# Two row combinations of a Winograd convolution move from GpSimd to VectorE

## The chip, the cores and the metric

The kernel runs on one core of a Trainium2 chip. A core has five engines with instruction queues of their own: TensorE (PE in the profile; PEld is its weight loading), VectorE (DVE), ScalarE (ACT), GpSimd (POOL) and SyncE (SP), which here only issues transfers. All tensors are float32. The metric is the time on the device in microseconds, as the median of several runs.

## The reference, cut to what matters

Four layers run one after the other on `x` of shape 2 x 128 x 128 x 128 (image, channel, row, column). Layers 0 and 2 are a 3x3 convolution followed by a small state-space recurrence and a group normalisation, layer 1 is a gating by local density. The change lies in layer 3, a basic block:

```
w1b = w1 + lax.stop_gradient(jnp.sign(w1) - w1)
w2b = w2 + lax.stop_gradient(jnp.sign(w2) - w2)
out = jax.nn.relu(_batchnorm(_conv3x3(x, w1b), gamma1, beta1))
out = _batchnorm(_conv3x3(out, w2b), gamma2, beta2)
out = out + x
return jax.nn.relu(out)
```

`_batchnorm` needs mean and variance over both images, so the first convolution has to be complete before the second begins. The input of layer 3 is the output of layer 2, `x + silu(groupnorm(...))`, and the kernel makes this sum band by band inside the first convolution.

## The kernel before, in words

Layer 3 is `_basic_block`. Channels lie on the 128 partitions. The 2 x 128 rows are cut into 32 bands of 8 rows (`BAND`), each two groups of four rows (`fours`). A band tile `xb` has 10 rows of 130 columns; three of them (`room`) are used in turn.

The 3x3 convolution is done by a Winograd scheme along the rows. For four output rows, six input rows are turned into six combinations (`comb`, the tile `v` of 6 x 2 x 130 elements a partition), each is multiplied by three weight matrices (one for each column tap) on TensorE, and the six products are put together into four output rows.

The combinations are made in three functions:

- `edges` (L889): VectorE makes four of them as `high - 4 * low` from rows of the band, one instruction of 260 elements each, and puts them at positions 0, 3, 2 and 5 of `v`.
- `differences`: GpSimd makes the two outer combinations in one instruction of 520 elements (L895: position 2 minus 0 and position 5 minus 3, written to 0 and 5), then a sum in place at position 3 (L896), then the differences at positions 1 and 4 straight from the band (L897).
- `rest_of` (L901 to L903): VectorE finishes positions 4, 1 and 2 from these.

`products` (L910) is the 18 matrix products of a band into `m` in PSUM (36 records in the profile). `conv` puts them together: ScalarE copies one third to `c` (L921), VectorE does four sums and differences (L925, L926), five steps into the result `Y` (L930 to L934) and two statistics (L936). `m` has two buffers in PSUM and `v` three in SBUF.

In the first convolution each band also has: `load` on SyncE's queue (L980 for the band, L982 for the residual's operand), and `residual`: ScalarE's Silu on the band (L988), GpSimd's addition of the residual (L989, 1280 elements), and SyncE's store of the sum (L990). In the second convolution there is `normalised` instead: GpSimd copies two rows (L1001) and ScalarE does the rest (L1003).

`convolve` writes the order out by hand for all five engines (`manual_schedule`): each engine gets its instructions in the order of the text. Step `k` finishes the combinations of band `k+1`, begins those of `k+2`, multiplies band `k`, puts band `k-1` together, and on GpSimd does the operations of `differences` for band `k+2` and then the residual of band `k+3`.

Of the kernel before, what the change touches and what calls it, by code (L numbers as in the profile page):

```python
# [27 lines left out]
ALU = mybir.AluOpType  # L28
# [791 lines left out]
def _basic_block(tc, src, y, norm, x3, scratch, w1, w2, bn, out, B, H):  # L820
# [7 lines left out]
    nc = tc.nc  # L828
    fours = BAND // 4
    with tc.tile_pool(name="bb", bufs=1) as cp, tc.tile_pool(name="bband", bufs=2) as bp, tc.tile_pool(  # L830
# [3 lines left out]
        def combined():  # L834
            return bp.tile([P, 6, fours, P + 2], F32, tag="comb", name="comb", bufs=3)
# [35 lines left out]
        def span(k):  # L871

            r0 = bands[k][1]
            return room[k % 3], 1 if r0 == 0 else 0, BAND + 1 if r0 + BAND == H else BAND + 2

        def border(k):
# [3 lines left out]
            if hi == BAND + 1:  # L880
                nc.gpsimd.memset(xb[:, BAND + 1, :], 0.0)

        def edges(k):

            xb = span(k)[0]
            v = combined()
            low, high = [xb[:, n : n + BAND, :].rearrange("p (i n) w -> p n i w", n=4) for n in (0, 2)]
            for n, at in enumerate((0, 3, 2, 5)):
                nc.vector.scalar_tensor_tensor(v[:, at], low[:, n], -4.0, high[:, n], ALU.mult, ALU.add)  # L889
            return v  # L890

        def differences(k, v):
            xb = span(k)[0]
            low, high = [xb[:, n : n + BAND, :].rearrange("p (i n) w -> p n i w", n=4) for n in (0, 2)]
            nc.gpsimd.tensor_tensor(v[:, 0:6:5], v[:, 2:6:3], v[:, 0:4:3], ALU.subtract)  # L895
            nc.gpsimd.tensor_tensor(v[:, 3], v[:, 2], v[:, 3], ALU.add)  # L896
            nc.gpsimd.tensor_tensor(v[:, 1:5:3], high[:, 1:3], low[:, 1:3], ALU.subtract)  # L897

        def rest_of(v):
            x = [v[:, n].rearrange("p i w -> p (i w)") for n in range(6)]  # L900
            nc.vector.scalar_tensor_tensor(x[4], x[1], -2.0, x[4], ALU.mult, ALU.add)  # L901
            nc.vector.scalar_tensor_tensor(x[1], x[1], 4.0, x[4], ALU.mult, ALU.add)
            nc.vector.scalar_tensor_tensor(x[2], x[2], 2.0, x[3], ALU.mult, ALU.subtract)  # L903

        def products(v):

            m = pp.tile([P, 3, 2, fours, P], F32, tag="m", name="m")
            for n, i in enumerate((2, 4, 3, 1, 0, 5)):
                for kw in range(3):
                    nc.tensor.matmul(  # L910
                        m[:, n // 2, n % 2],
                        lhsT=u[:, i, kw, :],
                        rhs=v[:, i, :, kw : kw + P],
                        start=(kw == 0),
                        stop=(kw == 2),
                    )
            return m

        def conv(m, b, r0, stats):
            c = bp.tile([P, 2, fours, P], F32, tag="c", name="c")  # L920
            nc.scalar.copy(c, m[:, 0])  # L921
            sd1 = bp.tile([P, 2, fours, P], F32, tag="sd", name="sd", bufs=1)
            sd2 = pp.tile([P, 2, fours, P], F32, tag="sd", name="sd")
            for n, sd in enumerate((sd1, sd2)):
                nc.vector.tensor_tensor(sd[:, 0], m[:, 1, n], c[:, n], ALU.add)  # L925
                nc.vector.tensor_tensor(sd[:, 1], m[:, 1, n], c[:, n], ALU.subtract)  # L926
            rows = Y[:, b, r0 : r0 + BAND, :]
            y = rows.rearrange("p (i n) w -> p n i w", n=4)
            (s1, d1), (s2, d2) = [(sd[:, 0], sd[:, 1]) for sd in (sd1, sd2)]
            nc.vector.tensor_tensor(y[:, 0:4:3], m[:, 2], sd1, ALU.add)  # L930
            nc.vector.scalar_tensor_tensor(y[:, 1], d2, 2.0, d1, ALU.mult, ALU.add)
            nc.vector.scalar_tensor_tensor(y[:, 2], s2, 4.0, s1, ALU.mult, ALU.add)
            nc.vector.tensor_tensor(y[:, 0], s2, y[:, 0], ALU.add)
            nc.vector.scalar_tensor_tensor(y[:, 3], d2, 8.0, y[:, 3], ALU.mult, ALU.add)  # L934
            for n in range(BAND // ROWS):
                nc.vector.bn_stats(  # L936
                    stats[:, (b * H + r0) // ROWS + n, :],
                    rows[:, n * ROWS : (n + 1) * ROWS, :].rearrange("p r w -> p (r w)"),
                )

        def affine(stats, n):
            mv = cp.tile([P, 2], F32, tag=f"mv{n}", name="mv")
            nc.vector.bn_aggr(mv, stats.rearrange("p a b -> p (a b)"))
            rstd = _rstd(nc, cp, mv[:, 1:2], BN_EPS, f"bn{n}")
            return _affine(nc, cp, mv[:, 0:1], rstd, bnc[:, 2 * n : 2 * n + 1], bnc[:, 2 * n + 1 : 2 * n + 2], f"bn{n}")
# [4 lines left out]
        def convolve(load, make, n):  # L950

            stats = cp.tile([P, B * H // ROWS, 6], F32, tag="st", name="st")
            v = {}
            E = mybir.EngineType
            with tc.manual_schedule(engines={E.PE, E.Activation, E.DVE, E.Pool, E.SP}):
                m = {}
                for k in range(-4, len(bands) + 1):
                    if 0 <= k + 1 < len(bands):
                        rest_of(v[k + 1])
                    if 0 <= k + 2 < len(bands):  # L960
                        v[k + 2] = edges(k + 2)
                    if 0 <= k < len(bands):
                        m[k] = products(v.pop(k))
                    if k >= 1:
                        conv(m.pop(k - 1), *bands[k - 1], stats)
                    if 0 <= k + 2 < len(bands):
                        differences(k + 2, v[k + 2])
                    for ahead, f in ((4, load), (3, make)):
                        if 0 <= k + ahead < len(bands):
                            f(k + ahead)  # L970
            return affine(stats, n)
# [12 lines left out]
        def residual(k):  # L984
# [5 lines left out]
            nc.sync.dma_start(out=x3[b][:, r0 : r0 + BAND, :], in_=xb[:, 1 : BAND + 1, 1 : P + 1])  # L990

        s1, t1 = convolve(load, residual, 0)


# [11 lines left out]

        nc.sync.dma_start(out=u.rearrange("p a t c -> p (a t c)"), in_=later)
        s2, t2 = convolve(lambda k: None, normalised, 1)

        for k, (b, r0) in enumerate(bands):  # L1010
# [11 lines left out]
def _program(ctx, tc, d, cols, out):  # L1022
# [7 lines left out]
    with tc.tile_pool(name="const", bufs=1) as cp, tc.tile_pool(name="wts", bufs=1) as wp:  # L1030
# [24 lines left out]
        with tc.tile_pool(name="ps_n", bufs=1, space=PSUM) as pp:  # L1055
            norm = [_norm(nc, npool, pp, w, con, stats, b) for b in range(B)]
    _basic_block(tc, x2, y, norm, x3, scratch, d["L3_w1"], d["L3_w2"], d["L3_bn"], out, B, H)


# [41 lines left out]
```

## Time and profile before

| | |
|---|---|
| runs shown | 7577.68 us median of 3 (7575.1 to 7587.97) |
| the profiled execution | 7595.04 us, span 7593.2 us |
| mean granted TensorE clock | 0.929 |
| the first convolution's combinations | 6928.9 us to 7205 us of the span |
| the second convolution | 7228 us to 7490 us |

Times inside the profile are microseconds from the start of the span. A row of instructions gives busy time, mean duration in ns, and the idle time of the engine before them with what ended it. In a timeline, "x36" means 36 instructions run together into one piece, and the bracket says how long the engine sat idle before and what released it. L12 is line 12 of the kernel.

### The profile page before, as it was taken

The numbers are of one execution on the slowest core, as the hardware profiler recorded it, in microseconds if no ns is written. First come the engines' busy times: TensorE is split into PE (matmuls) and PEld (weight loads), VectorE is DVE, ScalarE is ACT, GpSimd is POOL, SyncE is SP. The second block draws the span as 40 slices with busy tenths as digits, with TensorE's granted clock in tenths as the row PEclk, the third lists the DMA queues.
The fourth block names the chain that finished last, engine by engine and source line by source line (L and its number), as shares of the span: only waits on it lengthen the run. The fifth ranks groups of instructions, "written<-read, shape, count | busy, mean of one in ns | idle before, by whom it ended". The sixth has DMA issues, their size and how long they took to land.

```text
span 7593.2 us, 89536 instructions
## 1 busy us (share of the span) xinstructions
PE 6291.6 (83%) x30416; PEld 2339.8 (31%) x30416; DVE 7026.3 (93%) x7082; ACT 4279.0 (56%) x4877; POOL 5538.6 (73%) x1815
## 2 busy tenths in 40 slices
PE   7888888888888888867888888888888888887994
PEld 2222222222222222234222222222222222224773
DVE  6999999999999999968699999999999999998986
ACT  5566656666656666545566656665666566562222
POOL 5778777877787788743687787878777877785641
PEclk8999999999999999977899999999999999997997
DMA  7999999999999999954899999999999999996604
GB/s 207 247 248 250 252 245 251 252 253 249 247 252 255 248 250 253 251 183 173 211 256 245 248 244 248 251 253 246 248 252 248 251 248 246 247 256 184 194 7 172
DMA packets 573737, 1769.79 MB, mean 233 GB/s; under 512 B 85568, under 2 KB 239712, under 8 KB 458208
## 3 DMA queue, kind: packets, MB, share of 16 engines
q1 hardware_dynamic: 568672, 1747.28, 88.1%
q10 hardware_dynamic: 4608, 16.78, 0.6%
q8 instruction: 242, 3.96, 0.2%
q14 instruction: 215, 1.76, 0.1%
HBM read 1552.83 MB, written 210.89 MB: 232 GB/s over the span
## 4 chain that ended last, share of the span: by engine, by line
DVE 39%; DMA 30%; PE 14%; issue 6%; POOL 5%; ACT 4%; SPq 2%; POOLq 0%; DVEq 0%; ACTq 0%
DMA bcr<-sb 23%; DVE set L472 12%; DVE h L477 10%; DVE r L473 10%; DMA ur<-su 4%; PE m L910 4%; POOL h L445 3%; PE set L454 2%; PE one L350 2%; ACT set L463 2%; PE ys L492 1%; PE ys L483 1%; DVE v L505 1%; PE one L400 1%; DVE comb L901 1%
## 5 line engine op out<-in xcount | busy, mean ns | idle before, releaser
L445 POOL TENSOR_TENSOR h<-ur,bcr 128x2048 f32<-128x2048 f32 x896 | 4059.2, 4537 | 1331.9 <-DMA bcr<-sb 1098.7
L472 DVE TENSOR_TENSOR set<-set,h 128x1024 f32<-128x1024 f32 x1792 | 2192.5, 1223 | 257.4 <-ACT set L463 153.8
L473 DVE TENSOR_TENSOR r<-set,bcr 128x1024 f32<-128x1024 f32 x1792 | 2194.4, 1225 | 61.4
L463 ACT ACTIVATE set<-set 128x1024 f32<-128x1024 f32 x1792 | 1743.7, 1007 | 790.0 <-PE set L454 776.4
L477 DVE TENSOR_TENSOR h<-set,h 128x1024 f32<-128x1024 f32 x1536 | 1865.4, 1214 | 43.7 <-POOL h L445 43.1
L454 PE MATMUL set<-dt,rep 32*128 32x512 f32 x7168 | 1385.9, 676 | 97.8 <-DVE h L477 93.5
L492 PE MATMUL ys<-r,ct 128*32 128x512 f32 x7168 | 1160.1, 634 | 33.0 <-DVE r L473 32.6
L323 PE MATMUL one<-band,conv 128*128 128x512 f32 x2304 | 1083.5, 606 | 22.6 <-DMA band<-in_x_dram 12.3
L400 PE MATMUL one<-xc,keep 128*64 128x512 f32 x1008 | 314.8, 707 | 470.3 <-ACT xc L357 355.8
L454 PEld LDWEIGHTS set<-dt,rep 32*128 32x128 f32 x7168 | 403.1, 193 | 977.0 <-issue 478.0
L323 PEld LDWEIGHTS one<-band,conv 128*128 128x128 f32 x2304 | 407.7, 190 | 669.1 <-issue 597.1
L910 PE MATMUL m<-comb,u 128*128 128x256 f32 x2304 | 510.2, 382 | 63.0 <-DVE comb L903 45.3
L483 PE MATMUL ys<-t,ct 128*128 128x512 f32 x512 | 324.5, 720 | 252.1 <-DVE v L505 250.5
L910 PEld LDWEIGHTS m<-comb,u 128*128 128x128 f32 x2304 | 437.5, 191 | 135.4 <-issue 72.0
L492 PEld LDWEIGHTS ys<-r,ct 128*32 128x32 f32 x7168 | 181.2, 111 | 911.3 <-issue 756.9
L352 ACT ACTIVATE xc<-one,keep 128x512 f32<-128x512 f32 x252 | 173.3, 688 | 509.7 <-PE one L350 504.8
L420 PE MATMUL one<-prod,ct 128*128 128x512 f32 x504 | 284.7, 648 | 148.4 <-POOL prod L412 126.7
L374 POOL TENSOR_TENSOR u<-dt,xc 128x1024 f32<-128x1024 f32 x128 | 302.6, 2364 | 78.1 <-ACT dt L368 77.8
L350 PE MATMUL one<-y,w_in 128*128 128x512 f32 x504 | 340.7, 765 | 1.7 <-ACT xc L352 1.7
L421 ACT COPY t<-one 128x512 f32<-128x512 f32 x252 | 147.7, 586 | 326.9 <-PE one L420 326.9
L463 ACT ACT_TABLE_LOAD x254 | 325.9, 1283 | 4.5
L427 POOL TENSOR_TENSOR t<-t,xc 128x1024 f32<-128x1024 f32 x128 | 302.1, 2360 | 10.0
(166 smaller groups left out, 6116.2 us busy)
## 6 DMA issues: line engine op xcount, KB each, us to landing
ur<-su SPq DMA_DIRECT2D x896, 896.0 KB, 11.6
bcr<-sb SPq DMA_DIRECT2D x896, 448.0 KB, 11.8
ur<-su SPq DMA_DIRECT2D x896, 128.0 KB, 11.2
su<-u SPq DMA_DIRECT2D x1024, 64.0 KB, 3.2
sb<-bc SPq DMA_DIRECT2D x256, 224.0 KB, 2.7
bcr<-sb SPq DMA_DIRECT2D x896, 64.0 KB, 11.1
y<-o SPq DMA_DIRECT2D x128, 256.0 KB, 9.2
band<-in_x_dram SPq DMA_DIRECT2D x28, 640.0 KB, 11.0
```

What stands on the lines that cost most here:

```text
L323: nc.tensor.matmul(py.rearrange("p (r w) -> p r w", r=ROWS), lhsT=w["conv"][:, tap, :], rhs=xb[:, r + kh : r + kh + ROWS, kw : kw + P], st ...
L350: nc.tensor.matmul(p, lhsT=w[("in", "z")[i]][:, g, :], rhs=s["y"], start=True, stop=True)
L400: nc.tensor.matmul(p[g * NQ * DS : (g + 1) * NQ * DS, :], lhsT=w[("xb", "xcm")[i]], rhs=s["xc"][:, g, :], start=True, stop=True,)
L445: nc.gpsimd.tensor_tensor(b, s["ur", t], s["bc", t][:, 0].unsqueeze(1).to_broadcast([P, NJ, NS]), ALU.mult)
L454: nc.tensor.matmul(a[j // 2][:, j % 2, :], lhsT=w["rep"][r, q, :], rhs=s["dt"][r, g, :], start=True, stop=True, tile_position=(r.start, 0),)
L463: nc.scalar.activation(x, x, AF.Exp)
L472: nc.vector.tensor_tensor(pt, pt, s["h", t - 1][:, js, :], ALU.mult)
L473: nc.vector.tensor_tensor(s["r", t][:, js, :], pt, s["bc", t - 1][:, 1].unsqueeze(1).to_broadcast([P, 2, NS]), ALU.mult)
L477: nc.vector.tensor_tensor(s["h", t][:, js, :], pt, s["h", t][:, js, :], ALU.add)
L483: nc.tensor.matmul(s["ys", g], lhsT=con["ident"], rhs=s["t1"][:, g, :], start=True, stop=False)
L492: nc.tensor.matmul(s["ys", g][a : a + NQ * DJ, :], lhsT=red[:, q, :], rhs=r[:, j, :], start=False, stop=(q == NQ - 1), tile_position=(0, a),)
L910: nc.tensor.matmul(m[:, n // 2, n % 2], lhsT=u[:, i, kw, :], rhs=v[:, i, :, kw : kw + P], start=(kw == 0), stop=(kw == 2),)
```

## The change

GpSimd's instruction for the two outer combinations becomes a function of its own, `outer`, which takes the engine as an argument. In the first convolution (`n == 0`) it is issued on VectorE, directly behind the four instructions of `edges`. In the second (`n > 0`) it stays on GpSimd, and GpSimd's order there is what it was: outer combinations, sum, differences. The sum at position 3 moves from `differences` to the text of the loop.

```
+        def outer(engine, v):
+            engine.tensor_tensor(v[:, 0:6:5], v[:, 2:6:3], v[:, 0:4:3], ALU.subtract)
+
...
         def differences(k, v):
             xb = span(k)[0]
             low, high = [xb[:, n : n + BAND, :].rearrange("p (i n) w -> p n i w", n=4) for n in (0, 2)]
-            nc.gpsimd.tensor_tensor(v[:, 0:6:5], v[:, 2:6:3], v[:, 0:4:3], ALU.subtract)
-            nc.gpsimd.tensor_tensor(v[:, 3], v[:, 2], v[:, 3], ALU.add)
             nc.gpsimd.tensor_tensor(v[:, 1:5:3], high[:, 1:3], low[:, 1:3], ALU.subtract)
...
                     if 0 <= k + 2 < len(bands):
                         v[k + 2] = edges(k + 2)
+                        if n == 0:
+                            outer(nc.vector, v[k + 2])
                     if 0 <= k < len(bands):
                         m[k] = products(v.pop(k))
                     if k >= 1:
                         conv(m.pop(k - 1), *bands[k - 1], stats)
                     if 0 <= k + 2 < len(bands):
+                        if n > 0:
+                            outer(nc.gpsimd, v[k + 2])
+                        nc.gpsimd.tensor_tensor(v[k + 2][:, 3], v[k + 2][:, 2], v[k + 2][:, 3], ALU.add)
                         differences(k + 2, v[k + 2])
```

More of the change, by code (lines that the diff above doesn't have):

```diff
@@ L881, in border, with outer @@
                 nc.gpsimd.memset(xb[:, BAND + 1, :], 0.0)
+        def outer(engine, v):
+            engine.tensor_tensor(v[:, 0:6:5], v[:, 2:6:3], v[:, 0:4:3], ALU.subtract)
         def edges(k):
@@ L894, in differences @@
             low, high = [xb[:, n : n + BAND, :].rearrange("p (i n) w -> p n i w", n=4) for n in (0, 2)]
-            nc.gpsimd.tensor_tensor(v[:, 0:6:5], v[:, 2:6:3], v[:, 0:4:3], ALU.subtract)
-            nc.gpsimd.tensor_tensor(v[:, 3], v[:, 2], v[:, 3], ALU.add)
             nc.gpsimd.tensor_tensor(v[:, 1:5:3], high[:, 1:3], low[:, 1:3], ALU.subtract)
@@ L961, in convolve @@
                         v[k + 2] = edges(k + 2)
+                        if n == 0:
+                            outer(nc.vector, v[k + 2])
                     if 0 <= k < len(bands):
@@ L966, in convolve @@
                     if 0 <= k + 2 < len(bands):
+                        if n > 0:
+                            outer(nc.gpsimd, v[k + 2])
+                        nc.gpsimd.tensor_tensor(v[k + 2][:, 3], v[k + 2][:, 2], v[k + 2][:, 3], ALU.add)
                         differences(k + 2, v[k + 2])
```

## The prediction

> **What bounds the kernel now.** I read four views in this order: the page's engine line, then the table of windows over the last 700 us, then the timeline of one band in each of the two convolutions, then the rows of single instructions that have the shape of the moved one.
>
> The page's engine line says that VectorE (DVE) is the busiest engine of the whole program. It does not say where; over 90% of the span belongs to other stages, which the change doesn't touch.
>
> ```profile
> PE 6291.6 (83%) x30416; PEld 2339.8 (31%) x30416; DVE 7026.3 (93%) x7082; ACT 4279.0 (56%) x4877; POOL 5538.6 (73%) x1815
> ```
>
> The windows show the stage itself. Columns: the window, its length, then busy us and count of PE, PEld, DVE, ACT and POOL, the granted PE clock, the DMA share, GB/s. The first row lies in the first convolution, the second in the second one.
>
> ```profile
> 7080.00:7100.00 20.00, 18.24 (x83) 15.13 (x82) 19.76 (x43) 4.85 (x6) 14.58 (x12) 1.00 0.76 234
> 7340.00:7360.00 20.00, 20.00 (x95) 17.53 (x94) 18.76 (x47) 3.73 (x5) 10.64 (x12) 1.00 0.00 0
> ```
>
> First convolution: DVE is full (19.76 of 20) and TensorE (PE) has gaps. Second: PE is full and DVE has gaps. Both have the same matmuls, 36 records a band, so 95 records in 20 us against 83 to 87 is the price of being bound by DVE. DVE's fullness is partly false, though, as the timeline of one band of the first convolution shows (start, duration, engine, line; DVE, POOL and PE pieces, some left out):
>
> ```profile
> 7086.01 1.44 DVE L889 SCALAR_TENSOR_TENSOR comb<-band 128x260 f32<-128x260 f32 x4
> ...
> 7087.37 0.42 DVE L925 TENSOR_TENSOR sd<-m,c 128x256 f32<-128x256 f32 x1
> 7087.60 1.29 POOL L895 TENSOR_TENSOR comb<-comb 128x520 f32<-128x520 f32 x1 [2.59 <-DVE comb L889]
> ...
> 7088.84 0.68 DVE L930 TENSOR_TENSOR Y<-m,sd 128x512 f32<-128x512 f32 x1
> 7088.97 0.73 POOL L896 TENSOR_TENSOR comb<-comb 128x260 f32<-128x260 f32 x1
> ...
> 7089.66 1.30 POOL L897 TENSOR_TENSOR comb<-band 128x520 f32<-128x520 f32 x1
> 7089.66 8.01 PE L910 MATMUL m<-comb,u 128*128 128x256 f32 x36 [0.59 <-DVE Y L930]
> ...
> 7090.91 2.69 POOL L989 TENSOR_TENSOR band<-band,xs 128x1280 f32<-128x1280 f32 x1
> ...
> 7092.08 1.81 DVE L901 SCALAR_TENSOR_TENSOR comb<-comb 128x260 f32<-128x260 f32 x1
> ...
> 7093.92 0.43 DVE L902 SCALAR_TENSOR_TENSOR comb<-comb 128x260 f32<-128x260 f32 x1
> ...
> 7094.61 1.44 DVE L889 SCALAR_TENSOR_TENSOR comb<-band 128x260 f32<-128x260 f32 x4
> ```
>
> And the same two DVE instructions in the second convolution, where GpSimd (POOL) has no residual to add:
>
> ```profile
> 7344.57 0.41 DVE L901 SCALAR_TENSOR_TENSOR comb<-comb 128x260 f32<-128x260 f32 x1
> 7345.01 0.43 DVE L902 SCALAR_TENSOR_TENSOR comb<-comb 128x260 f32<-128x260 f32 x1
> ```
>
> A band takes 8.60 us, from L889 to L889. L901 takes 0.41 us when POOL is quiet and 1.81 us here: it begins while POOL's residual L989 runs (7090.91 to 7093.60) and L902 begins 0.32 us after that ends. So of the 8.60 us, L901 to L902 is 1.84 instead of 0.44: 1.40 us a band in which DVE stands, booked as busy. PE waits for DVE (0.59 us before L910, for L930). Through this stage the chain is DVE's, and one of its links is POOL's residual, whose end is set by the three POOL operations in front of it.
>
> **The change part by part.** I count time in a band from the first L889 (7086.01 is 0). Before: L925 at 1.36, L895 at 1.59, L896 at 2.96, L897 at 3.65, L989 from 4.90 to 7.59, L901 at 6.07, L902 at 7.91, next L889 at 8.60.
>
> *Added to DVE: 32 instructions of 128x520 from two SBUF tiles.* No DVE row has just this shape; two bracket it:
>
> ```profile
> L853 DVE TENSOR_TENSOR comb<-comb 128x384 f32<-128x384 f32 x2 | 1.1, 551 | 0.0
> L847 DVE TENSOR_TENSOR comb<-comb 128x1152 f32<-128x1152 f32 x2 | 2.7, 1358 | 0.7 <-ACT comb L846 0.6
> ```
>
> (mean ns is the number behind the comma). Between them 768 elements cost 0.807 us, 1.05 ns each, so 520 elements last 0.551 + 136 x 1.05 = 0.69 us. The next instruction starts before the end of one: L930, 0.68 long, is followed after 0.60, so the queue pays 0.61. It reads what the fourth L889 wrote just before: where L902 reads what L901 wrote the step is 0.44 instead of the 0.34 between independent ones, so 0.10 more. Cost on DVE: 0.71 us a band, all of it on the chain. Nothing hides it.
>
> Here a rule of the Trainium skill speaks against the change. The page "Vector Engine (DVE) Microarchitecture Reference", section "Points that are easy to get wrong", says that the scalar_tensor_tensor with two SBUF sources that are not bf16 runs at half throughput. Taken over to this operation, that is about 0.07 + 2 x 0.54 + 0.10 = 1.25 us instead of 0.71 (an estimate from that page). The rows say otherwise: L889 is such an instruction and takes 0.42 us for 260 elements, against 0.41 for 256 in L931, which has one source in PSUM; and L847 above has two f32 SBUF sources at 1.05 ns an element. I take 0.71 and keep 1.25 as the upper end. I see no reason for less than 0.61.
>
> *Removed from POOL: L895, 1.29 us, in the first convolution only.* The sum (L896) now waits for DVE's new instruction, because it overwrites what that reads. Behind it in POOL's queue stand the difference (L897), which needs only the band, and the residual; behind the residual, SyncE's queue has the store L990 and the next band's loads L980 and L982. The new instruction runs from 1.46 to 2.15. POOL began 0.15 after the last L889's end before; the same hand-over gives 2.30 for the sum. With the old steps (0.69 from L896 to L897, 1.25 from L897 to L989) the difference starts at 2.99, the residual at 4.24, and it ends at 6.93 instead of 7.59: 0.66 us earlier.
>
> *What becomes of the stall.* L901 starts 0.71 later, at 6.78. If free, L902 follows at 7.22; behind the residual it follows at 6.93 + 0.32 = 7.25. So 1.40 us of stall shrink to 0.03, and the two conditions are nearly level. Next L889 at 7.25 + 0.69 = 7.94. The band goes from 8.60 to 7.94: **0.66 us less.** Two things moved by the same edit: 0.71 of work added, 1.37 of stall gone.
>
> A second rule bears on it: "SBUF — State Buffer", section "SBUF: two separate sides", says that a DVE instruction with two SBUF inputs and a GpSimd instruction exclude each other for the whole of whichever starts first. The L901 row above agrees. By the rule the new instruction is one more that must find POOL idle, or loses up to the residual's 2.68 us. By the timeline POOL is idle from the residual's end to the sum, 6.93 to 10.24 in the new count (the band is 7.94), and L902, L903, the four L889 and the new one all lie in it. So the rule adds nothing here, but it names the condition.
>
> *What is late next.* PE needs 7.77 us a band: in the second convolution, with PE full, L895 comes at 7347.86 and 7355.63. So 7.94 leaves PE 0.17 us of gap, and 0.66 is nearly all that can be had (0.83 at most). DMA: after L990 (7085.03) the next load goes out at 7085.49, the activation on it ends at 7092.59, and the residual that uses it comes at 7099.50: 6.9 us in hand. With the shorter band it is 2 x 0.66 less, 5.6 us. The copy L921 runs a band ahead of L925. DVE's L889 needs the comb tile of three bands back, freed by PE long before.
>
> *Ends of the stage.* The first three L901 (2.9 us each) wait for L897 and then through the residual; their bands are 8.48 and 8.51 long and become 7.94 by the same steps: 1.1 us for two, and some 0.4 for the very first, whose L901 waits for the same POOL chain. From 6957.39 to 7197.58 there are 28 whole bands: 28 x 0.66 = 18.5. In the last one that makes combinations (L889 at 7197.58) no residual remains and the 0.71 is a pure cost in front of L930, which releases PE's last 15.78 us. The second convolution keeps POOL's three operations in their order: nothing. Sum: 18.5 + 1.1 + 0.4 - 0.7 = **19.3 us.**
>
> The sum is made against the profiled execution, 7595.04 us with a span of 7593.2, which is 0.23% above the median of the runs shown. The loop that it cuts is paced by engines and not by that excess, so I take it from the median: 7577.7 - 19.3 = 7558.4, rounded to 7558.
>
> **The rivals.**
>
> *A, TensorE becomes the bound (6%).* If the new instruction pays no 0.10 for its operand and L901 comes free, DVE needs 8.60 - 1.40 + 0.61 = 7.81, and with hand-overs either engine gives about 7.8: 0.8 x 28 + 1.5 - 0.6 = 23 us, 7554. For it: the two engines are level within 0.2 us. Against: the 0.10 is in every dependent pair of the timeline.
>
> *B, part of the stall stays (8%).* The sum now waits for a different engine's last word each band. If it starts 0.35 us later than worked out, L902 is 0.35 later, the band gains 0.31: 28 x 0.31 + 1.5 - 0.7 = 9.5 us, 7568. Each 0.1 us of delay at the sum costs 2.8 us. Against: L895 has waited for DVE in the same way, always with 0.14 to 0.15.
>
> *C, the half rate of the skill's rule (5%).* 1.25 us on DVE, residual ends at 7.47, L902 at 7.79, band 8.48: 28 x 0.12 + 0.5 - 1.25 = 3 us less, 7575. Against: the rows above.
>
> *D, slower (5%): the residual is not ready when POOL comes to it.* Place: L989 waiting for the activation L988, which waits for its load. Then the residual slides onto L901 to L889 and the new instruction and holds all of them back. It decides when the residual ends later than before, so 0.66 us after the place worked out; at 1.5 us late the band is 9.44, 0.84 x 28 = 23 us more, 7601. For it: L988 waits for DMA in nearly every band already. Against: the 5.6 us in hand.
>
> That the change doesn't do what it says is little to be feared: the order on the five engines in this loop is the order of the text.
>
> **How the numbers follow.** The forecast has 76%. Its own spread is some 4 us (0.05 us a band is 1.4 us; runs shown differ by 12.9 us, a median by less). The 0.2% bound, about what a measurement of this kernel can tell from no change, is 15 us, one such spread short of 19.3, so 86% of the forecast counts as faster: 0.76 x 0.86 + 0.06 = 0.71. Within: 0.76 x 0.14 + 0.08 + 0.05 = 0.24. Slower: 0.05. The range goes from 7549 (A with a low median) to 7574 (B, and nearly to C); it leaves out D and most of C.
>
> **What would show it.** L889 to L889 in steady bands 7.94 us (8.60 before). A new DVE row comb<-comb 128x520 x32 at 0.69 us, and only 32 of POOL's 1.29. L901 in the first convolution from 1.8 to about 0.5 us. L902 within 0.35 us of the end of L989. PE's gap before L910 from 0.59 to about 0.2. Page: DVE busy down by some 20 us, POOL down by 41. The second convolution still at 7.77. I am wrong if the new row is above 0.8 us, if L901 stays above 1 us, or if the granted clock in this stage falls below 1.00 with PE at 98%; 20 us windows of the second convolution, at 100%, show 1.00.

## The result, and the profile after

The changed kernel takes 7564.94 us (median of 22 runs) against 7584.77 us before (22 runs beside them). The ratio is 0.9973, with a 95% interval of 0.9965 to 0.9981. That is 19.8 us less (14 to 27 by the interval), where 19.3 were forecast. The absolute forecast of 7558 is 7 us low because the median before was 7 us higher here than in the three runs it was counted from. Line numbers move: the four edge instructions are now L892, `outer` is L884, the sum L972, the difference L898, the residual L995, and `rest_of` L902 to L904 (before: L901 to L903).

The page's engine line, after:

```profile
PE 6319.0 (83%) x30416; PEld 2335.1 (31%) x30416; DVE 7011.8 (93%) x7114; ACT 4282.3 (57%) x4877; POOL 5499.8 (73%) x1783
```

VectorE has 32 instructions more and is busy 14.5 us less; GpSimd has 32 less and is busy 38.8 us less. Work was added to an engine and its busy time fell, which is possible only where busy time contained waiting.

The windows, after, one of each convolution (columns as before):

```profile
7080.00:7100.00 20.00, 20.00 (x92) 16.77 (x91) 19.66 (x49) 4.58 (x5) 12.06 (x9) 1.00 0.82 246
7340.00:7360.00 20.00, 20.00 (x94) 17.53 (x93) 18.77 (x48) 3.45 (x4) 10.77 (x12) 1.00 0.01 1
```

In the first convolution VectorE now does 49 instructions in 20 us instead of 43 and is as full as it was. The second convolution is what it was.

One band of the first convolution in the timeline, after:

```profile
7086.93 1.44 DVE L892 SCALAR_TENSOR_TENSOR comb<-band 128x260 f32<-128x260 f32 x4
...
7088.40 0.70 DVE L884 TENSOR_TENSOR comb<-comb 128x520 f32<-128x520 f32 x1
7089.02 0.42 DVE L926 TENSOR_TENSOR sd<-m,c 128x256 f32<-128x256 f32 x1
7089.25 0.74 POOL L972 TENSOR_TENSOR comb<-comb 128x260 f32<-128x260 f32 x1 [3.32 <-DVE comb L884]
...
7089.94 1.30 POOL L898 TENSOR_TENSOR comb<-band 128x520 f32<-128x520 f32 x1
...
7091.19 2.69 POOL L995 TENSOR_TENSOR band<-band,xs 128x1280 f32<-128x1280 f32 x1
...
7093.73 0.44 DVE L902 SCALAR_TENSOR_TENSOR comb<-comb 128x260 f32<-128x260 f32 x1
...
7094.20 0.43 DVE L903 SCALAR_TENSOR_TENSOR comb<-comb 128x260 f32<-128x260 f32 x1
...
7094.89 1.44 DVE L892 SCALAR_TENSOR_TENSOR comb<-band 128x260 f32<-128x260 f32 x4
```

From L892 to L892 is 7.96 us. `outer` starts 1.47 after the first edge instruction, GpSimd's sum 2.32 after, the residual 4.26 after; it ends at 7093.88, and L903 starts 0.32 later. L902 lasts 0.44 instead of 1.81. Two rows carry the rest, the new instruction and the one that stood in the queue (the second row has the 32 of the stage and one of the second convolution; its mean contains the three start-up bands of 2.9 us):

```profile
L884 DVE TENSOR_TENSOR comb<-comb 128x520 f32<-128x520 f32 x32 | 22.4, 700 | 1.1
L902 DVE SCALAR_TENSOR_TENSOR comb<-comb 128x260 f32<-128x260 f32 x33 | 22.1, 671 | 9.8 <-POOL comb L898 9.8
```

Where the time went, from the starts in the two traces. The 28 whole bands: 240.19 us before (6957.39 to 7197.58), 223.12 after (6951.50 to 7174.62), 17.07 less. The two start-up bands: 16.99 before, 15.73 after, 1.26 less. The first: 0.54 less. From the last edge instructions to the aggregation of the statistics: 24.96 before, 25.69 after, 0.73 more. Together 18.1 us. The span of the profiled execution shrank by 21.7 us; the rest is scatter in stages that the change does not touch (the first edge instructions came 4.1 us earlier after, and the end took back 0.5).

### The profile page after: what moved, and what is told of

The parts are those of the page before. It is cut to its first block, busy times and chain, and to the rows that moved or that the text cites. A ratio compares the mean times of both kernels' runs of the same rounds, so it can differ in the third digit from the quotient of the medians.

```text
span 7571.5 us, 89536 instructions
## 1 busy us (share of the span) xinstructions
PE 6319.0 (83%) x30416; PEld 2335.1 (31%) x30416; DVE 7011.8 (93%) x7114; ACT 4282.3 (57%) x4877; POOL 5499.8 (73%) x1783
## 4 chain that ended last, share of the span: by engine, by line
DVE 41%; DMA 25%; PE 19%; issue 7%; ACT 5%; POOL 2%; SPq 1%; POOLq 0%; DVEq 0%; ACTq 0%
DMA bcr<-sb 19%; DVE set L472 14%; DVE h L477 12%; DVE r L473 12%; PE m L911 6%; DMA ur<-su 3%; PE one L350 2%; PE set L454 2%; ACT set L463 2%; PE ys L492 2%; PE one L400 2%; POOL h L445 2%; DVE v L505 1%; PE ys L483 1%; ACT xc L357 1%
## 5 line engine op out<-in xcount | busy, mean ns | idle before, releaser
L454 PE MATMUL set<-dt,rep 32*128 32x512 f32 x7168 | 1402.9, 675 | 104.9 <-DVE h L477 98.1
L911 PE MATMUL m<-comb,u 128*128 128x256 f32 x2304 | 507.8, 381 | 46.0 <-DVE comb L904 44.8
L911 PEld LDWEIGHTS m<-comb,u 128*128 128x128 f32 x2304 | 436.2, 190 | 117.3 <-issue 54.5
L364 PE MATMUL one<-xc,w_dt 128*128 128x512 f32 x504 | 306.4, 692 | 2.7 <-ACT bc L407 2.7
```

Source lines behind the costliest of these rows:

```text
L454: nc.tensor.matmul(a[j // 2][:, j % 2, :], lhsT=w["rep"][r, q, :], rhs=s["dt"][r, g, :], start=True, stop=True, tile_position=(r.start, 0),)
L911: nc.tensor.matmul(m[:, n // 2, n % 2], lhsT=u[:, i, kw, :], rhs=v[:, i, :, kw : kw + P], start=(kw == 0), stop=(kw == 2),)
```

## The experiments

All are judged by the trace first: the length of a steady band is good to about 0.01 us there, while a few us of the whole time drown in its scatter. e5_memset, e6_read, e7_sums, e9_gate and e10_sums2 ran once each, so only their traces count and no ratio is given. The "stage" is the time from the first instruction of `rest_of` to the aggregation of the first convolution's statistics: 285.8 us before, 268.1 after.

Theory P says that in this stage what is short is neither engine alone but the two together, the pair: GpSimd's instructions that read SBUF and VectorE's instructions with two SBUF operands take turns, and the band is the sum of the turns. Rival Q says that GpSimd's queue matters only for when the combinations are ready. Rival R is what the page of the changed kernel itself suggests: its chain of waits, asked over the steady bands alone, names TensorE for everything.

```profile
6959.79 83.72 PE m L911 x379
7043.51 0.10 issue
7043.61 126.50 PE m L911 x572
```

**e1_both: VectorE's new work without GpSimd's relief.**

```
+                        if n == 0:
+                            w = v[k + 2]
+                            nc.gpsimd.tensor_tensor(w[:, 1:5:3], w[:, 2:6:3], w[:, 0:4:3], ALU.subtract)
                         nc.gpsimd.tensor_tensor(v[k + 2][:, 3], v[k + 2][:, 2], v[k + 2][:, 3], ALU.add)
```

> The changed kernel, but in the first convolution GpSimd keeps an instruction as long as the one it gave away (same three operands, written to positions 1 and 4, which the difference overwrites right after). So VectorE's 0.71 us is added and nothing is taken from GpSimd. Theory P (the pair): GpSimd's instructions and VectorE's two-SBUF instructions take turns, and the band is their sum: 7.96 + 1.37 = 9.33 us a band, some 24 us slower than before. Rival Q (the queue): what matters is when GpSimd has the combinations ready for L902, not when its residual ends; they are still ready in time (5.67 against 6.78), so the band stays near 7.96. Rival R (TensorE sets 7.96): unchanged at 7.96 or a little over.

Measured: 9.32 us a band, stage 308.4 us, ratio to before 1.0025 (1.0013 to 1.0038). P to 0.01 us; Q and R fall. The timeline shows the residual starting later and L902 held again, although the combinations it needs were ready at 7096.22:

```profile
7094.92 1.30 POOL L898 TENSOR_TENSOR comb<-band 128x520 f32<-128x520 f32 x1
7096.18 2.68 POOL L998 TENSOR_TENSOR band<-band,xs 128x1280 f32<-128x1280 f32 x1
7097.35 1.79 DVE L902 SCALAR_TENSOR_TENSOR comb<-comb 128x260 f32<-128x260 f32 x1
```

**e2_half: half the residual, nothing else, in the kernel before.**

```
-            nc.gpsimd.tensor_tensor(x, x, rests.pop(k), ALU.add)
+            half = rests.pop(k)
+            nc.gpsimd.tensor_tensor(x[:, :, : P // 2], x[:, :, : P // 2], half[:, :, : P // 2], ALU.add)
```

> The kernel before, with the residual added on 64 of the 128 columns only (half of that sum is left out); nothing else. GpSimd's L989 should take about 1.35 us instead of 2.69. P: L901 is held 1.34 us less, the turns add up to 7.26, VectorE alone needs 7.18 to 7.2, so TensorE's 7.77 is the band: 24 us faster than before. Q: the residual stands behind the combinations in GpSimd's queue, so nothing changes, 8.60.

Measured: 7.33 to 7.36 us a band in the first eight steady bands and 7.77 in the last nineteen; stage 259.4 us, 26.4 less than before in the trace. The half residual took 1.43 us, not 1.35, and 8.60 - (2.69 - 1.43) = 7.34 is the sum of the turns in the early bands. That TensorE's 7.77 does not bind there, because it had run ahead, is argued and not shown; the second convolution, too, has a few bands of 7.20 before it settles at 7.77. The ratio is 0.9978 (0.9970 to 0.9987), which is 17 us and at most 23, less than the stage gained. In this trace the second convolution (268.9 us against 269.0) and what follows it are as before, so the rest does not lie behind the stage; the runs do not say where it lies.

Q falls: GpSimd's combinations are ready no sooner, and the band is shorter all the same. The four edge instructions do read the residual's result, but in the steady bands they start 1.0 us or more after its end, here and in the kernel before, so that is not the wait either. TensorE's floor of 7.77 shows as VectorE waiting for it, which the changed kernel never does in its steady bands:

```profile
7145.79 1.43 POOL L990 TENSOR_TENSOR band<-band,xs 128x640 f32<-128x640 f32 x1
7146.95 0.56 DVE L901 SCALAR_TENSOR_TENSOR comb<-comb 128x260 f32<-128x260 f32 x1
...
7148.65 1.45 DVE L889 SCALAR_TENSOR_TENSOR comb<-band 128x260 f32<-128x260 f32 x4 [0.34 <-PE m L910]
```

**e5_memset and e6_read: which GpSimd instruction holds VectorE off.** One line behind the residual, in the kernel before, on a spare tile `idle`:

```
             nc.gpsimd.tensor_tensor(x, x, rests.pop(k), ALU.add)
+            nc.gpsimd.memset(idle, 0.0)                                                          # e5, 1000 elements
+            nc.gpsimd.tensor_tensor(idle[:, :260], idle[:, :260], idle[:, 260:520], ALU.add)     # e6
```

> The kernel before with a GpSimd memset of 1000 elements into a spare tile behind each residual (it reads nothing from SBUF; a memset of 130 elements takes 0.2 us, so some 0.5 to 1 us). P with the page's clause that only a GpSimd instruction that reads SBUF holds VectorE off: L901 goes on when the residual ends, the memset lies in GpSimd's 2.59 us of idle time, band 8.60. If any GpSimd instruction holds VectorE off: the band grows by the memset, to 9.1 to 9.6.

> The kernel before with a GpSimd addition of 260 elements (two SBUF inputs, spare tile) behind each residual. Nothing waits for its result. P: L901 stays held until it ends, 0.69 us a band more, 9.29. Q, and any theory in which VectorE waits for results: it lies in GpSimd's idle time, 8.60.

Measured: e5_memset 8.59 us a band, as before; e6_read 9.00. In e5_memset VectorE's instructions go on at their usual length while the memset of 0.94 us runs:

```profile
7091.86 1.81 DVE L903 SCALAR_TENSOR_TENSOR comb<-comb 128x260 f32<-128x260 f32 x1
7093.32 0.94 POOL L992 MEMSET idle<- 128x1000 f32 x1
7093.70 0.43 DVE L904 SCALAR_TENSOR_TENSOR comb<-comb 128x260 f32<-128x260 f32 x1
```

So GpSimd's additions, which read SBUF, hold VectorE off, and the memset, which only writes, does not, as the Trainium skill has it ("SBUF — State Buffer", "SBUF: two separate sides"). Nobody reads the result of the addition in e6_read, so no theory in which VectorE waits for data explains its longer band. The size in e6_read was off, 0.41 instead of 0.69, and its timeline says why:

```profile
7083.92 2.68 POOL L991 TENSOR_TENSOR band<-band,xs 128x1280 f32<-128x1280 f32 x1
7084.95 1.94 DVE L903 SCALAR_TENSOR_TENSOR comb<-comb 128x260 f32<-128x260 f32 x1
7086.56 0.92 POOL L992 TENSOR_TENSOR idle<-idle 128x260 f32<-128x260 f32 x1
7086.93 0.84 DVE L904 SCALAR_TENSOR_TENSOR comb<-comb 128x260 f32<-128x260 f32 x1
```

(L903 and L904 are the first two of `rest_of` in both kernels.) The waiting L903 got its turn between the two GpSimd instructions: it ended 0.29 us after the residual. GpSimd's addition then took 0.92 instead of the 0.73 that the same shape takes elsewhere, which reads as a wait for VectorE in its turn, and L904 was held until 0.29 after it. I had counted L903 as held through both; where VectorE gets in between two of GpSimd's instructions, the plain sum of the turns is too long, here by 0.29 us.

**e7_sums and e10_sums2: less work on VectorE outside the turns.** Both reorder the four sums and differences of `conv` in the changed kernel (the code is e10_sums2's; e7_sums comes to the order in the comment):

```
-            for n, sd in enumerate((sd1, sd2)):
-                nc.vector.tensor_tensor(sd[:, 0], m[:, 1, n], c[:, n], ALU.add)
-                nc.vector.tensor_tensor(sd[:, 1], m[:, 1, n], c[:, n], ALU.subtract)
+            for n, i in ((1, 0), (0, 0), (0, 1), (1, 1)):       # e10; e7: (1, 0), (0, 0), (1, 1), (0, 1)
+                nc.vector.tensor_tensor((sd1, sd2)[n][:, i], m[:, 1, n], c[:, n], (ALU.add, ALU.subtract)[i])
```

> The changed kernel with the four sums and differences of conv in another order (second add, first add, second subtract, first subtract), so that the step of 0.46 us between the two that write PSUM becomes 0.34: VectorE's own work per band drops by about 0.1 us, in both convolutions, outside the turns with GpSimd. P: the band of the first convolution stays at 7.96, since L902 still waits for the end of the residual, then for longer (0.1 us more). If VectorE's own work is the bound: 7.86. R: 7.96, and L902 not held.

> The changed kernel with the four sums and differences in the order second add, first add, first subtract, second subtract. e7_sums took the 0.12 us from one step and gave it to the next, because the last one wrote what L931 reads; here it does not, so VectorE's own work drops by 0.11 us a band, outside the turns. P: the first convolution stays at 7.96, L902 held for 0.15 us. VectorE's own work as the bound: 7.85.

Measured: 7.97 and 7.96. e7_sums says nothing, because it saved no work: the step from its last difference to L931, which reads what that wrote, grew to 0.45 us. e10_sums2 did save it, and the band did not move; L902 took the 0.13 us back by being held that much longer:

```profile
7100.65 0.57 DVE L902 SCALAR_TENSOR_TENSOR comb<-comb 128x260 f32<-128x260 f32 x1
```

So in the changed kernel VectorE's own work does not bind, though VectorE is busy 19.66 us of 20.

**e8_rest and e11_rest_sums: less work inside the turns.** e8_rest exchanges two lines in the changed kernel, and e11_rest_sums is e8_rest and e10_sums2 together:

```
             nc.vector.scalar_tensor_tensor(x[4], x[1], -2.0, x[4], ALU.mult, ALU.add)
-            nc.vector.scalar_tensor_tensor(x[1], x[1], 4.0, x[4], ALU.mult, ALU.add)
             nc.vector.scalar_tensor_tensor(x[2], x[2], 2.0, x[3], ALU.mult, ALU.subtract)
+            nc.vector.scalar_tensor_tensor(x[1], x[1], 4.0, x[4], ALU.mult, ALU.add)
```

> The changed kernel with the last two instructions of rest_of exchanged, so that none reads what the one just before it wrote: 0.1 us a band less in VectorE's work, and inside the turns with GpSimd. P and VectorE's own work: 7.86 us a band in the first convolution, 3 us in all. R: 7.96. Second convolution unchanged at 7.77, TensorE's.

> e8_rest and e10_sums2 together. P: the turns stay at e8_rest's 7.84 us a band, L902 held a little. VectorE's own work as the bound: 7.73, so TensorE's 7.77. Between these ends lie 2 us of the whole, so the time will not tell them apart, the trace will.

Measured: 7.84 us a band in both; stages 264.2 and 263.8 us. Ratios to before 0.9971 (0.9959 to 0.9982) and 0.9964 (0.9955 to 0.9972). R falls here, too: nothing was taken from TensorE, yet the band is 0.12 us shorter, and TensorE has 94 records in 20 us (e8_rest, below) instead of 92. In e11_rest_sums L902 lasts 0.57 instead of 0.44: VectorE's further saving went into a longer hold, as in e10_sums2.

```profile
7080.00:7100.00 20.00, 20.00 (x94) 17.56 (x93) 19.73 (x51) 4.43 (x5) 10.09 (x9) 1.00 0.76 228
```

TensorE reads 20.00 of 20 here and in the changed kernel, probably because the profile models the end of a matmul: in the kernel before, where the gap is wide enough to show, the 36 matmuls of a band are booked at 8.01 us instead of 7.77, and 0.24 us more would cover a gap of 0.2. e11_rest_sums has the lowest ratio of all runs, and in the trace its stage is 4.3 us shorter than the change's. The intervals overlap, so the times alone do not tell it from the change.

**e3_sum and e9_gate: the sum on VectorE too.**

```
                             outer(nc.vector, v[k + 2])
+                            nc.vector.tensor_tensor(v[k + 2][:, 3], v[k + 2][:, 2], v[k + 2][:, 3], ALU.add)
...
-                        nc.gpsimd.tensor_tensor(v[k + 2][:, 3], v[k + 2][:, 2], v[k + 2][:, 3], ALU.add)
+                            nc.gpsimd.tensor_tensor(v[k + 2][:, 3], v[k + 2][:, 2], v[k + 2][:, 3], ALU.add)
+                        if n == 0:                                                           # e9 only
+                            nc.gpsimd.tensor_copy(idle, v[k + 2][:, 3, 0, :2])               # e9 only
                         differences(k + 2, v[k + 2])
```

> The changed kernel with the sum at position 3 (260 elements) moved to VectorE as well, right behind the outer combinations, in the first convolution. P: GpSimd's residual now ends at about 6.7 us in the band, before L902 is due at 7.2, so the turns no longer bind, but VectorE's own work does: 7.93 + 0.34 + 0.10 for the operand = 8.37 us a band; 11 us slower than the change, still 6 to 8 us faster than before. R: TensorE still sets 7.96, no difference from the change.

Measured: slower than before, ratio 1.0022 (1.0009 to 1.0034), 8.9 and 9.7 us a band in turn, 9.3 on average, stage 305.5 us. My expectation of 8.37 was wrong. The timeline shows GpSimd's difference starting late, on TensorE's word:

```profile
7058.90 1.44 DVE L892 SCALAR_TENSOR_TENSOR comb<-band 128x260 f32<-128x260 f32 x4
...
7062.53 1.29 POOL L898 TENSOR_TENSOR comb<-band 128x520 f32<-128x520 f32 x1 [4.63 <-PE m L911]
...
7064.37 2.42 POOL L996 TENSOR_TENSOR band<-band,xs 128x1152 f32<-128x1152 f32 x1 [0.56 <-ACT band L995]
...
7066.16 0.91 DVE L902 SCALAR_TENSOR_TENSOR comb<-comb 128x260 f32<-128x260 f32 x1
```

Moving the sum away took from GpSimd's queue the instruction that waited for VectorE, and the difference then waited until 3.6 us into this band for the end of a product. (In most other bands the profile names no releaser, but there, too, the difference starts within 0.1 us of ScalarE's copy of a finished product.) e9_gate puts a two-element read of VectorE's sum in front of it and changes nothing else.

> e3_sum, with a GpSimd copy of two elements of VectorE's sum put in front of the difference, so that GpSimd's queue starts on VectorE's word again, as in the change, and not on TensorE's. If the late start of the difference on TensorE (3.6 to 4.6 us into the band instead of 2.3) is what made e3_sum slow, the band falls to VectorE's own 8.37 (up to 8.45 with the small copy's hand-over). If moving the sum itself is what costs, it stays at 9.3.

Measured: 8.40 us a band, stage 280.6 us, the first instruction of `rest_of` free at 0.41 us.

```profile
7073.90 0.18 POOL L976 COPY idle<-comb 128x2 f32<-128x2 f32 x1 [4.41 <-DVE comb L966]
7074.04 1.29 POOL L899 TENSOR_TENSOR comb<-band 128x520 f32<-128x520 f32 x1
```

So the late start was the cause, and with it gone VectorE's own work binds at 8.40, with no instruction held: the sum is one instruction too many for VectorE. Why the difference's wait points at that product was not tried; that it is the release of the three-fold `comb` buffer, which VectorE's instructions wait for on GpSimd's behalf in the other kernels, is only argued.

**e4_second: the change in both convolutions.**

```
-                        if n == 0:
-                            outer(nc.vector, v[k + 2])
+                        outer(nc.vector, v[k + 2])
...
-                        if n > 0:
-                            outer(nc.gpsimd, v[k + 2])
```

> The change made in both convolutions. In the second one GpSimd has no residual and VectorE no stall, so there is nothing to win: VectorE's work goes from some 7.2 to 7.9 us a band, past TensorE's 7.77. P: 7.9 us a band there instead of 7.77, 4 to 6 us slower than the change. Q: GpSimd's queue gets shorter, so no loss, 7.77. First convolution as with the change, 7.96.

Measured: 7.93 us a band in the second convolution instead of 7.77, but its start-up bands go from 6.27 to 5.65 (they wait for GpSimd's combinations), so the second convolution as a whole is 2.4 us longer than the change's (270.1 against 267.7 us from one aggregation to the other). Ratio to before 0.9982 (0.9974 to 0.9989). The steady part went as P says; the start-up I had left out. Times alone do not tell it from the change.

## Why the prediction was right

Point by point, by its own steps:

- *The stall is L901 behind the residual, 1.40 us a band.* Right: halving the residual (e2_half) takes L901 from 1.81 to 0.56 us, an addition behind it (e6_read) holds the next instruction too, and a memset (e5_memset) holds nothing.
- *0.71 us of work added.* Right: 0.70 long, 0.62 to the next start, 0.11 for the operand, 0.73 in all. The half rate (1.25) does not show here: the row says 700 ns for 520 elements.
- *GpSimd's sum 0.15 after `outer`, residual from 4.24 to 6.93.* It ran from 4.26 to 6.95.
- *A band of 7.94.* 7.96. But the saving of 0.66 was read from one band of 8.60; over the 28 bands the mean before is 8.58, after 7.97, with the bands at the border between the images in it. So 17.1 us instead of 18.5 is the term that was too large, and the start (1.8 instead of 1.5) gave a little back. The trace's 18.1 is the figure to hold against the forecast; that the measured 19.8 came within 0.5 us of 19.3 is luck, given an interval of 14 to 27.
- *0.7 us lost at the end of the stage.* 0.73.
- *VectorE's busy time down by some 20 us.* 14.5. The first three L902 of the stage are held for 2.9 us as before, so some 4 us of stall that were counted as gone are still there.
- *TensorE and the transfers stay out of it.* Right: granted clock 1.00 in both rows, and in e2_half, where TensorE runs at its 7.77, the windows show 1.00 too. The residual never waited for its activation in the steady bands. A gap of 0.2 us before L911, which I said would show, is not shown, for the reason given under e8_rest.

None of the four rivals came: the operand's 0.11 us was paid (A), the sum started on time (B), the rate was full (C), and the residual found its activation done (D).

What the prediction had not said is that its numbers are the sum of the turns. Before: 1.37 + 0.69 + 1.25 + 2.69 on GpSimd, hand-overs of 0.15 and 0.32, 0.69 for the end of `rest_of` and 1.44 for the edges, which makes 8.60. After: 1.37 out, 0.71 in. The saving is the difference of what one operation costs on the two engines, 0.66 us, because both take turns.

That the two conditions came out level (7.22 and 7.25) is chance: the stall of 1.40 us happened to be about as long as the 1.37 that left GpSimd's queue. VectorE's own work with the new instruction is 7.93 us a band (the second convolution of e4_second, where nothing holds it), the turns are 7.96. By these figures the change would have won hardly more had the operation taken longer on GpSimd, because VectorE's own work would then have been the bound.

## What to carry to other kernels

Where an instruction takes several times its usual time, and only while another engine runs, add up the instructions of the two engines that exclude each other, with the hand-overs between them: that sum can be the period, even when each engine's own work fits. Moving an operation inside such a sum pays by the difference of its durations, until the receiving engine's own work becomes the longer (here 7.97 with one operation moved, 8.40 with two). And when an instruction is moved off a queue, look at what the next one in that queue waits for.

## What I had not expected of the hardware

- In e6_read a VectorE instruction that was held off got in between two GpSimd additions that stood back to back, and the second of these took 0.92 us instead of 0.73. In the start-up bands, where VectorE arrived 0.07 us after the residual had begun, it was held for the whole of it (2.88 us).
- In e5_memset a GpSimd memset of 0.94 us cost VectorE's two-operand instructions beside it nothing (0.43 us, as without it).
